# Row sums of squares by four transposes and a VectorE sum, and another order of products in the feed-forward blocks

## The chip, the core and the metric

The kernel runs on one core of a Trainium2 chip. The metric is the device time of one execution in microseconds (us), the median of several runs. All arithmetic is in fp32. In the profile PE is the matrix engine (TensorE), PEld its weight loads, DVE is VectorE, ACT is ScalarE, POOL is GpSimd and SP is the engine that issues most of the DMAs.

## The reference

The input x has four samples of 512 tokens with 256 features. Cut to what matters:

```python
# attention part, on n = layernorm(x)
q = silu(n @ Wq1 @ Wq2); a = exp(log_sigmoid(sigmoid(n @ Wk1 @ Wk2))); k = 1 - a; v = n @ Wv
h = scan over tokens of  h = a * h + k * v
out = q * h                                                     # 512 features per token
out = out * rsqrt(mean(out * out, -1) + 1e-6) * norm_w          # a sum of squares per token
x = x + layernorm(out @ Wo)
# feed-forward part, six blocks
y = layernorm(x)
for i in range(6):
    y = gelu(y @ W1[i].T + B1[i]) @ W2[i].T + B2[i] + y         # 256 -> 1024 -> 256 features
    if i < 5: y = layernorm(y) * LN_G[i] + LN_B[i]
x = x + layernorm(y)
```

## The kernel before

Features lie on the partitions and a sample's 512 tokens along the free dimension, except where a layer norm needs tokens on the partitions.

**Attention.** Each sample b is an object `Attention(b)`. `k1_q1`, `value(e)` and `scan(e)` make the four 128-feature parts e of `out` (the tile `ht`) and of its squares `sq`; GpSimd adds the four squares parts into one 128x512 tile, `self.sq[-1]`. `output(t)` multiplies the part of 128 tokens t by Wo, into one of two PSUM buffers `pt` that are used in turn. `residual()` (line 911) then needs the sum of squares of each token. It makes it by four products of a 128x128 slice of `sq[-1]` with a column of ones (line 917), which leaves a 128x4 tile in a `pt` buffer, and VectorE turns that into `ve` (line 920). A chain on GpSimd (`rstd_of`), ScalarE (`normalized`), GpSimd (the sum with x) and VectorE (`token_stats`) follows, and at its end the normalized sample is passed through DRAM (`passage`: VectorE block transposes, one store and four loads by SP) into the feature layout, where `ffn_input` picks it up. The sample's work is interleaved with that of the next one.

**Feed-forward.** The four samples go in two groups g of two samples (1024 tokens). For each block i and group g, an object `Hidden(i, g)` makes the hidden layer by 26 block products in place of 32, in the way of Strassen's method: `A_SUMS` are sums of blocks of W1, `B_SUMS` are sums of blocks of the input (both on GpSimd; `input_sums(g)` writes the tiles `tx`), and `RESULT` lists the products (p), the copies and partial sums (v) and the results (h). A line `p6 += s13 t8` is two PE products, each over one half of a 128x512 PSUM bank, added onto what the bank holds. A line `v14 = p6` is a ScalarE copy of the bank (line 497), a line `v13 = v8 + p6` a VectorE sum (line 514) that reads the bank. When both halves of a row's tokens are there, ScalarE applies gelu (line 495), and VectorE or GpSimd makes sums t1 to t4 of the gelu results. `Output(i, g, hidden)` then makes the second layer by seven groups of four products, p1 to p7, in the order of `ORDER`, and the results go through DRAM to the layer norm (`Norm`) and back to the features.

**The order.** Nothing is issued at once. Each operation is recorded in `Plan` with a cost, and `Plan.run` emits them engine by engine: whichever of an engine's ready operations has the earliest latest-start time goes first. `AFTER` is how long after the last product the other engines may end in that calculation. The order in which operations are recorded decides which buffers they get, and so what waits for what: `DEFER` is how many products of `Output` are recorded only with the next `Hidden`; `HEAD` and `BY` say how these are mixed with its first steps. Engines run their emitted instructions in order, so a waiting instruction holds up those behind it.

Of the kernel before, what the change touches and what calls it, by code (L numbers as in the profile page):

```python
# [13 lines left out]
ALU = mybir.AluOpType  # L14
PSUM = bass.MemoryType.PSUM

P = 128
# [2 lines left out]
RMS_EPS = 1e-6  # L20
LAST_PARTS = (2 * P, 2 * P)
LAST_COLUMNS = (P, P)
ORDER = "p1 p2 p6 p7 p5:0 p4 p5:1 p5:23 p3".split()
LAST_ORDER = "p1 p2 p6 p7 p4 p5".split()
DEFER = 4
HEAD, BY = 1, (2, 1)
POOLROWS = (1, 2)
AFTER = 10.0
LAST_WAYS = "POOL POOL ACT DVE DVE".split()
WARM = 5  # L30
FIRST = ((0,), (1,), (2, 3))
# [7 lines left out]
s1 = a10 + a11  # L39
# [7 lines left out]
s9 = s3 + a31  # L47
s10 = s4 - a20
s11 = s6 - s0
s12 = s2 - a01  # L50
s13 = s5 + a10
s14 = a30 - s3
s15 = s2 + a21
s16 = a30 + a20
s17 = s4 - a00
s18 = a11 - a21
# [4 lines left out]
t1 = b13 - b12  # L61
# [3 lines left out]
t5 = b03 - t2  # L65
t6 = b02 - t0
t7 = b00 + b01
t8 = b03 - t1
t9 = b11 - t1
t10 = t7 - t1  # L70
t11 = b02 - t8
t12 = t2 - t3
t13 = t3 - b03
t14 = b00 - t5
t15 = b13 - b03
t16 = b12 - t6
t17 = b10 - t4
# [3 lines left out]
RESULT = """  # L81
p0 = a21 b10
v1 = p0
p4 = a20 b00
v8 = p4
h20 = v1 + p4
p1 = s1 t1
v2 = p1
p2 = s8 b12
v3 = p2  # L90
v4 = v2 - p2
p0 += s15 t2
v5 = p0
p3 = s0 t3
# [5 lines left out]
p3 += s2 t12  # L100
v10 = v6 - p3
p4 += s10 t7
h21 = v9 - p4
h22 = v10 + p4
p3 += a20 t13
h23 = v5 - p3
v12 = p3
p5 = a00 b00
# [3 lines left out]
p7 = s3 t0  # L112
v16 = v1 - p7
h11 = v15 + p7
p6 = s5 t15
v13 = v8 + p6
v14 = p6
p8 = a01 b10
h00 = v11 + p8
p9 = s7 b11  # L120
h01 = v15 + p9
p7 += s9 t6
v17 = p7
p6 += s13 t8
h13 = v4 + p6
p7 += s14 b02
h31 = v7 - p7
v20 = p7
p5 += s18 t17
h10 = v16 + p5  # L130
p6 += a10 t11
h12 = p6 - v3
v18 = v17 + p6
p8 += s12 t5
v19 = v12 + p8
h33 = v19 - v14
p8 += s16 t14
h30 = p8 - v13
p11 = s11 b03
h03 = v19 + p11  # L140
p10 = a31 t16
# [117 lines left out]
class Plan:  # L259
# [32 lines left out]
    def latest(self):  # L292

        last = [1e9] * len(self.ops)
        at = sum(cost for engine, cost, *_ in self.ops if engine == "PE")
        end = at + AFTER
        for n in reversed(range(len(self.ops))):
# [59 lines left out]
def kernel(  # L357
# [27 lines left out]
    nc = tc.nc  # L385
    B, S, E = x.shape
    HD, E2 = wq2.shape
    NB, _, HID = w1t.shape
    NT = S // P
# [12 lines left out]
    plan = Plan()  # L402
# [7 lines left out]
    def tile_of(name, shape):  # L410
        return tiles(name, shape)[0]
# [8 lines left out]
    ones = tile_of("ones", [P, 1])  # L420
# [81 lines left out]
    def on(engine):  # L502
        return {"DVE": nc.vector, "POOL": nc.gpsimd}[engine]

    def tt(engine, dst, a, b, alu):
        cost = 0.14 + 0.00213 * dst.size if engine == "POOL" else 0.07 + 0.00104 * dst.size
        if alu == ALU.pow:
            cost = 0.29 + 0.18 * dst.size
        elif engine == "DVE" and not in_psum & {id(v.bufs[0]) for v in (a, b)}:
            cost += 0.4  # L510
        plan.op(
            engine,
            cost,
            lambda: on(engine).tensor_tensor(dst.ap, a.ap, b.ap, alu),  # L514
            [a, b],
            [dst],
        )

    def tscalar(engine, dst, src, s0, s1, op0, op1=None):
        by = [s.ap if isinstance(s, View) else s for s in (s0, s1)]  # L520
        kw = {} if op1 is None else {"op1": op1}
        cost = 0.15 + 0.003 * dst.size if engine == "POOL" else 0.07 + 0.001 * dst.size
        plan.op(
            engine,
            cost,
            lambda: on(engine).tensor_scalar(dst.ap, src.ap, *by, op0, **kw),  # L526
            [src, *(s for s in (s0, s1) if isinstance(s, View))],
            [dst],
        )
# [11 lines left out]
    def product(dst, lhs, rhs, start):  # L541

        plan.op(
            "PE",
            max(0.858 * rhs.size / 512, 0.224),
            lambda: nc.tensor.matmul(  # L546
                dst.ap, lhs.ap, rhs.ap, start=start, stop=True, skip_group_check=True
            ),
            [lhs, rhs],
            [dst],  # L550
        )

    def transpose(dst, src):
        plan.op(
            "PE",
            0.107,
            lambda: nc.tensor.transpose(dst.ap, src.ap, ident.ap),  # L557
            [src],
            [dst],
        )  # L560
# [13 lines left out]
    def store(dst, src, engine="SP"):  # L574
        queue = nc.sync if engine == "SP" else nc.scalar
        kept = isinstance(dst, View)
        to = dst.ap if kept else dst
        plan.op(
            engine,
            0.45,  # L580
            lambda: queue.dma_start(out=to, in_=src.ap),
            [src],
            [dst] if kept else [],
            src.size * P * 4 / 0.26e6,
        )
# [101 lines left out]
    def token_stats(mv, src, t):  # L687

        st = sts.next()

        def emit():
            nc.vector.bn_stats(st.ap, src.ap)  # L692
            nc.vector.bn_aggr(mv.ap[:, t, :], st.ap)  # L693

        plan.op("DVE", 0.55, emit, [src], [st, mv])

    def rstd_of(mv, to, of=None, lo=0, hi=NT, negative=True):

        ve, r, nm, nb = (to[:, k, lo:hi] for k in range(4))
        if of is None:  # L700
            tscalar("POOL", ve, mv[:, lo:hi, 1], LN_EPS, None, ALU.add)
        else:
            tt("POOL", ve, of[:, lo:hi], mv[:, lo:hi, 1], ALU.add)
        tt("POOL", r, ve, neg_half[:, lo:hi], ALU.pow)
        if not negative:
            return r
        tscalar("POOL", nm, mv[:, lo:hi, 0], -1.0, None, ALU.mult)
        tt("POOL", nb, nm, r, ALU.mult)
        return r, nb

    def normalized(src, by, t):

        r, nb = by
        z = nns.next()
        to = z
        if len(src.ap.shape) == 3:
            to = z.with_ap(z.ap.rearrange("p (f r) -> p f r", r=src.ap.shape[2]))
        act(to, src, AF.Identity, nb[:, t : t + 1], r[:, t : t + 1])
        return z
# [66 lines left out]
    class Attention:  # L786
# [124 lines left out]
        def residual(self):  # L911

            pss = pts.next()
            for t in range(NT):
                product(pss[:, t : t + 1], self.sq[-1][:, ts(t, P)], ones, True)
            hts.back(*self.grids)
            ve = rs.next()[:, 0, :]
            tscalar(  # L920
                "DVE",
                ve,
                pss[:, :NT],
                LN_EPS / E2,
                LN_EPS * RMS_EPS,
                ALU.mult,
                ALU.add,
            )
            by = rstd_of(self.mv, rs.next(), of=ve)
            mv1 = mvs.next()  # L930
            for t in range(NT):
                z = normalized(self.y[t // 2][:, t % 2, :], by, t)
                x1 = xs[self.b][t]
                tt("POOL", x1, x1, z, ALU.add)
                token_stats(mv1, x1, t)
                store(kept[self.b][t], x1)
            self.x1_by = rstd_of(mv1, rs.next())
# [115 lines left out]
    class Output:  # L1053


        def __init__(self, i, g, hidden, cols=slice(0, S), parts=None):
# [10 lines left out]
            self.x = xts[g]  # L1067
            order = LAST_ORDER if self.ending else ORDER
            self.left = [(part[:2], int(j)) for part in order for j in part[3:] or "0123"]
# [272 lines left out]
    for i in range(NB):  # L1342
        for g in range(NG):
# [32 lines left out]
            for u in range(4):  # L1376
                output.take(2)
                norm.features(u)
            output.take(len(output.left) - DEFER)
            of = (i, g)  # L1380
# [69 lines left out]
```

## Time and profile before

| | |
|---|---|
| median of 3 runs | 678.9 us (678.58 to 680.04) |
| the profiled execution's own time | 679.37 us |
| its span in the profile | 677.6 us |
| PE busy | 667.7 us, 99% of the span |
| POOL, DVE, ACT busy | 562.1, 458.6 and 357.8 us |
| mean granted PE clock | 0.997 |
| products with the column of ones | 16, as 32 matmul records of 128x1 |
| transposes by PE | 32 records of 128x128 |

A product in fp32 is two matmul records in the profile, a transpose is one. The records overlap, since they are pipelined: a 512 column record lasts 592 ns but the next one starts 429 ns later. What PE costs is therefore read from start to start and not from the durations. A label such as `bank<-tx,sa` says which tile is written from which; all products have line 546, all transposes line 557, most VectorE and GpSimd sums line 514.

### The profile page before, as it was taken

To read this page: it belongs to the slowest core of one execution; us is meant where nothing else is said; L and a number is where in the kernel's file an instruction comes from. 1 tells how busy PE (TensorE), PEld (TensorE's weight loads), DVE (VectorE), ACT (ScalarE), POOL (GpSimd) and SP (SyncE) were. 2 spreads that over 40 slices of the span, in tenths; PEclk is the share of its full clock that TensorE was granted. 3 is DMA by queue.
4 is the path that set the end of the run, shared out by engine and by line. 5 is a ranking of instruction groups with operands and counts; after the bars stand their busy time and mean duration, and the time that the engine had idled before them with its cause. 6 is when DMAs were issued, how large, how long until landed. Compare 5 with 4: busy or idle time off the path is not lost.

```text
span 677.6 us, 8284 instructions
## 1 busy us (share of the span) xinstructions
PE 667.7 (99%) x2406; PEld 445.8 (66%) x2406; DVE 458.6 (68%) x878; ACT 357.8 (53%) x625; POOL 562.1 (83%) x718
## 2 busy tenths in 40 slices
PE   8999999999999999999999999999999999999995
PEld 7565558747648558467476485584674764855884
DVE  5567665866937848649569378496495693784955
ACT  3847767635725646438257256364382572563631
POOL 4999569967999859998589998599985899885874
PEclk9999999999999999999999999999999999999998
DMA  7500522134253141550432531516504306216501
GB/s 229 192 1 32 155 63 78 48 125 124 81 184 108 56 160 34 196 164 14 145 105 92 180 101 57 161 33 202 162 10 141 107 31 190 91 65 189 151 32 63
DMA packets 81838, 73.74 MB, mean 109 GB/s; under 512 B 6272, under 2 KB 70784, under 8 KB 81792
## 3 DMA queue, kind: packets, MB, share of 16 engines
q1 hardware_dynamic: 81504, 72.94, 33.6%
q8 instruction: 19, 0.31, 0.2%
q10 hardware_dynamic: 288, 0.26, 0.1%
q14 instruction: 27, 0.22, 0.1%
HBM read 43.82 MB, written 29.36 MB: 108 GB/s over the span
## 4 chain that ended last, share of the span: by engine, by line
PE 96%; ACT 1%; DMA 1%; DVE 1%; SPq 0%; issue 0%; POOLq 0%; DVEq 0%; POOL 0%
PE bank L546 91%; PE pt L546 5%; DMA w<-in_wv 1%; ACT ht L495 0%; SPq L568 0%; ACT n L495 0%; DVE st L692 0%; PE bank L557 0%; PE pt L557 0%; DVE bank L526 0%; DVE n L536 0%; DVE mv L693 0%; DVE ht L514 0%; POOLq L1446 0%; ACT tmp L497 0%
## 5 line engine op out<-in xcount | busy, mean ns | idle before, releaser
L546 PE MATMUL bank<-tx,sa 128*128 128x256 f32 x672 | 160.9, 379 | 0.0
L497 ACT COPY tmp<-bank 128x512 f32<-128x512 f32 x144 | 83.7, 583 | 143.4 <-PE bank L546 128.1
L546 PEld LDWEIGHTS bank<-tx,sa 128*128 128x128 f32 x672 | 127.5, 190 | 22.2 <-issue 3.8
L514 DVE TENSOR_TENSOR ht<-tmp,bank 128x512 f32<-128x512 f32 x156 | 101.0, 678 | 35.2 <-ACT tmp L497 17.4
L514 POOL TENSOR_TENSOR tc<-ht,tc 128x512 f32<-128x512 f32 x96 | 121.4, 1279 | 4.1 <-ACT ht L495 3.2
L495 ACT ACTIVATE ht<-ht,b 128x512 f32<-128x512 f32 x168 | 112.9, 714 | 15.8 <-DVE ht L514 14.5
L546 PE MATMUL bank<-tc,w 128*128 128x512 f32 (+1 forms) x216 | 95.2, 577 | 0.0
L546 PE MATMUL bank<-ht,sb 128*128 128x512 f32 (+2 forms) x208 | 88.1, 555 | 0.0
L546 PE MATMUL bank<-tc,sb 128*128 128x512 f32 (+2 forms) x208 | 86.7, 556 | 0.0
L514 DVE TENSOR_TENSOR tmp<-tmp,bank 128x512 f32<-128x512 f32 x96 | 63.5, 677 | 32.2 <-PE bank L546 17.9
L536 DVE SCALAR_TENSOR_TENSOR tmp<-bank,b,xt 128x512 f32<-128x512 f32 (+1 forms) x52 | 36.5, 702 | 71.6 <-PE bank L546 71.6
L546 PE MATMUL bank<-ht,w 128*128 128x512 f32 (+1 forms) x200 | 83.8, 568 | 0.3 <-ACT ht L495 0.3
L514 POOL TENSOR_TENSOR tx<-xt,tx 128x256 f32<-128x256 f32 x108 | 76.0, 732 | 0.9
L546 PEld LDWEIGHTS bank<-tc,sb 128*128 128x128 f32 x208 | 39.2, 190 | 42.9 <-issue 41.6
L546 PEld LDWEIGHTS bank<-tc,w 128*128 128x128 f32 x216 | 40.7, 190 | 39.9 <-issue 37.3
L495 ACT ACTIVATE n<-x,r 128x256 f32<-128x256 f32 x90 | 47.9, 588 | 34.7 <-POOL r L514 34.7
L546 PEld LDWEIGHTS bank<-ht,w 128*128 128x128 f32 x200 | 37.3, 190 | 39.4 <-issue 28.7
L514 POOL TENSOR_TENSOR tx<-xt 128x256 f32<-128x256 f32 x24 | 17.5, 729 | 53.8 <-ACT xt L495 44.5
L546 PEld LDWEIGHTS bank<-ht,sb 128*128 128x128 f32 x208 | 39.0, 190 | 33.2 <-issue 31.6
L546 PE MATMUL bank<-tx,w 128*128 128x256 f32 (+1 forms) x240 | 57.4, 366 | 0.5 <-DMA w<-in_wv 0.5
L514 DVE TENSOR_TENSOR tmp<-bank,tmp 128x512 f32<-128x512 f32 (+2 forms) x54 | 35.3, 654 | 24.2 <-PE bank L546 17.9
L546 PE MATMUL bank<-xt,sa 128*128 128x256 f32 x192 | 49.3, 379 | 0.0
(94 smaller groups left out, 1029.8 us busy)
## 6 DMA issues: line engine op xcount, KB each, us to landing
x<-passed SPq DMA_DIRECT2D x120, 128.0 KB, 3.0
passed<-x SPq DMA_DIRECT2D x16, 512.0 KB, 2.6
passed<-x SPq DMA_DIRECT2D x28, 256.0 KB, 2.3
room<-passed SPq DMA_DIRECT2D x56, 128.0 KB, 3.1
w<-in_w1t SPq DMA_DIRECT2D x6, 1024.0 KB, 4.9
w<-in_w2t SPq DMA_DIRECT2D x6, 1024.0 KB, 5.7
passed<-room SPq DMA_DIRECT2D x16, 256.0 KB, 2.1
passed<-room SPq DMA_DIRECT2D x6, 512.0 KB, 2.6
```

Source lines behind the costliest of these rows:

```text
L495: lambda: nc.scalar.activation(dst.ap, src.ap, func, **kw)
L497: else nc.scalar.copy(dst.ap, src.ap),
L514: lambda: on(engine).tensor_tensor(dst.ap, a.ap, b.ap, alu),
L536: lambda: nc.vector.scalar_tensor_tensor(dst.ap, a.ap, by, b.ap, op0, op1),
L546: lambda: nc.tensor.matmul(dst.ap, lhs.ap, rhs.ap, start=start, stop=True, skip_group_check=True),
```

## The change

In `residual()` the four products with ones become four transposes of the same slices, which fill a whole 128x512 PSUM buffer with tokens on the partitions, and VectorE sums over the 128 columns of each of the four parts into `ve`. Then the scaling by constants runs on `ve` in place. The list of products, `ORDER`, `DEFER`, `HEAD`, `BY` and `AFTER` change as well, which gives every engine another order in the feed-forward blocks; the products themselves are the same.

```diff
-ORDER = "p1 p2 p6 p7 p5:0 p4 p5:1 p5:23 p3".split()
+ORDER = "p1 p2 p6 p5:0 p7 p5:123 p4 p3".split()
-DEFER = 4
-HEAD, BY = 1, (2, 1)
+DEFER = 3
+HEAD, BY = 2, (4, 1)
-AFTER = 10.0
+AFTER = 6.0
...
 p0 = a21 b10
 v1 = p0
+p1 = s1 t1
+v2 = p1
 p4 = a20 b00
 v8 = p4
 h20 = v1 + p4
-p1 = s1 t1
-v2 = p1
...
 p4 += s10 t7
+h22 = v10 + p4
 h21 = v9 - p4
-h22 = v10 + p4
...
 p6 = s5 t15
 v13 = v8 + p6
 v14 = p6
+p6 += s13 t8
+h13 = v4 + p6
 p8 = a01 b10
 h00 = v11 + p8
+p7 += s9 t6
+v17 = p7
+p5 += s18 t17
+h10 = v16 + p5
 p9 = s7 b11
 h01 = v15 + p9
-p7 += s9 t6
-v17 = p7
-p6 += s13 t8
-h13 = v4 + p6
+p8 += s12 t5
+v19 = v12 + p8
+h33 = v19 - v14
+p6 += a10 t11
+h12 = p6 - v3
+v18 = v17 + p6
+p8 += s16 t14
+h30 = p8 - v13
 p7 += s14 b02
 h31 = v7 - p7
 v20 = p7
-p5 += s18 t17
-h10 = v16 + p5
-p6 += a10 t11
-h12 = p6 - v3
-v18 = v17 + p6
-p8 += s12 t5
-v19 = v12 + p8
-h33 = v19 - v14
-p8 += s16 t14
-h30 = p8 - v13
 p11 = s11 b03
 h03 = v19 + p11
...
             for t in range(NT):
-                product(pss[:, t : t + 1], self.sq[-1][:, ts(t, P)], ones, True)
+                transpose(pss[:, ts(t, P)], self.sq[-1][:, ts(t, P)])
             hts.back(*self.grids)
             ve = rs.next()[:, 0, :]
+            by_tile = pss.ap.rearrange("p (t f) -> p t f", f=P)
+            plan.op(
+                "DVE",
+                0.07 + 0.00104 * S,
+                lambda: nc.vector.tensor_reduce(
+                    out=ve.ap, in_=by_tile, op=ALU.add, axis=mybir.AxisListType.X
+                ),
+                [pss],
+                [ve],
+            )
             tscalar(
                 "DVE",
                 ve,
-                pss[:, :NT],
+                ve,
                 LN_EPS / E2,
                 LN_EPS * RMS_EPS,
                 ALU.mult,
```

## The prediction

> **What bounds the kernel now.** I read the page first, then PE's timeline at a few places, then the chain that ended last and the timelines of the engines around it.
>
> ```profile
> PE 667.7 (99%) x2406; PEld 445.8 (66%) x2406; DVE 458.6 (68%) x878; ACT 357.8 (53%) x625; POOL 562.1 (83%) x718
> ```
>
> PE is the bound, and the page cannot say how tightly, because records overlap. I therefore compared start to start: in long runs of equal records a 512 column record costs 0.429 us, a 256 column one 0.2155 and a transpose 0.109. With these, PE loses time after its first products only at the places named below; its last record starts at 670.35 us, and the 7.2 us behind it belong to DVE, POOL and the last stores. So a microsecond less on PE is a microsecond, unless something else is late then. PE's timeline at a residual of sample 0, and at two sets of transposes in sample 1's first norm:
>
> ```profile
> 47.26 1.45 PE L546 MATMUL bank<-tc,w 128*128 128x512 f32 x3
> 48.55 0.95 PE L546 MATMUL pt<-ones,ht 128*128 128x1 f32 x8
> 49.36 1.96 PE L546 MATMUL bank<-tc,w 128*128 128x512 f32 x4
> ...
> 23.59 0.60 PE L557 MATMUL pt<-ident,n 128*128 128x128 f32 x4
> 24.03 1.88 PE L546 MATMUL bank<-tc,w 128*128 128x512 f32 x4
> 25.75 0.60 PE L557 MATMUL pt<-ident,n 128*128 128x128 f32 x4
> ```
>
> The first column is the start. The four products with ones hold PE from 48.55 to 49.36, 0.81 us, and the four records behind them take 1.96 where they take 1.88 behind transposes: 0.89 us in all. Four transposes hold it from 23.59 to 24.03, 0.44 us.
>
> The largest hole in the middle of the run is at the first output products of block 0, group 0:
>
> ```profile
> 131.34 2.74 PE L546 MATMUL bank<-ht,w 128*128 128x512 f32 x6
> 134.36 2.84 PE L546 MATMUL bank<-ht,w 128*128 128x512 f32 x6 [0.29 <-ACT ht L495]
> ```
>
> Six records should end their turn at 131.34 + 6 x 0.429 = 133.91, the next starts at 134.36: 0.45 us lost, and 0.10 in the next six (2.84 for 2.74). The chain that ended last says why:
>
> ```profile
> 126.86 0.70 DVE ht L514
> 127.56 0.02 issue
> 127.58 0.59 ACT tmp L497
> 128.17 1.49 ACT n L495 x3
> 129.65 2.09 ACT ht L495 x4
> ```
>
> ScalarE's queue is full of norms and gelus there, and the gelu of `h30`, the last product's result, comes last. `p1:3` waits for it.
>
> **The change part by part.** Sums are against the profiled execution's own 679.37 us (span 677.6, 1.8 around it); the median of the runs is 678.9, 0.47 less.
>
> *Transposes.* Four residuals, 0.89 - 0.44 = 0.45 us less each: **-1.8 us**. All four stand where PE is never idle. The rows are of the same instruction with another source tile, so I take the price as firm to 0.1 us each. Against it speaks the Trainium skill, "TensorE: Matmul & The Clock Gate", Part 4: about 275 ns for a transpose in a kernel, and a transpose does not keep PE's clock up. The trace has 272 to 301 ns as duration but 109 ns from start to start, and the windows around the transposes at 22 to 27 us show a granted clock of 1.00. By the page's 275 ns the sixteen would cost 4.4 us, which is more than the 3.6 they replace; the trace decides.
>
> *VectorE's sum.* Four new instructions of 128x512 from PSUM. No row shows this operation. A statistics instruction over 128x256 takes 413 ns, an elementwise one on 128x512 from PSUM 678, a scan over 128x512 1212; between 0.4 and 1.2 I take 0.68, as the row with the same elements and source. It lengthens the residual's chain by that. Queued behind it on DVE are `stt`, `tt` and `scan` of the next sample, whose banks PE wants 4.3 to 5.9 us after they are free, and in sample 3 `v15`, needed 3.45 us after the transposes and ready about 1.6 after them. So on PE's path: 0. The pt buffer is held longer: the next user but one, `output(1)` of the next sample, comes 3.0 us after the transposes, against 0.3 + 0.68. The chain ends in sample 1's features, which the first hidden products read. There PE waits for `ffn_input1` with 0.42 us to spare, but that ScalarE copy starts at 101.78 behind three scan activations, while its data landed at 100.5. In the new order it goes ahead of them, and GpSimd does sample 1's second norm ahead of two `input_sums`. PE comes there 1.3 us earlier plus 0.86 for `p1` being moved up. Bounds 0 to 0.8; I take **+0.3** together with the same chain of samples 2 and 3 at group 1.
>
> *Block 0's hole.* In the new list `p8 += s16 t14` stands before `p7 += s14 b02`, `p11` and `p10`. So `h30` and `h31` have 1.7 to 2.2 us more before p1 starts, and their gelu is queued ahead of the others'. Laid out on the rows (0.6 us per sum, 0.7 per gelu), it is ready 1.2 us before `p1:3`. **-0.55** (0 to -0.55). What is late next there is GpSimd's t2 for `p6:0`, by the same rows 1.2 us early.
>
> *The last block.* Between 638 and 649 us PE loses 0.43 us at five waits of the same kind, for example at `h30`:
>
> ```profile
> 643.34 2.99 PE L546 MATMUL bank<-ht,w 128*128 128x256 f32 x12
> 646.17 0.59 PE L546 MATMUL pt<-ht,w 128*128 128x256 f32 x2
> ```
>
> Twelve records should be done at 645.93; PE goes on at 646.17. The waits for `h30`, `h13` and `v19` get 0.4 to 0.9 us more room; one for `v14` comes in. **-0.3** (0 to -0.43). Behind it the order on PE and DVE from the first `finish` on is the old one, and the 7.2 us after PE's last record stay. `AFTER` only sets priorities.
>
> *A new wait.* `p6 += s13 t8` moves up by one product pair, in front of `p9`: it now stands 1.72 us behind `p6 = s5 t15` in place of 2.59. Before it may add to the bank, DVE (`v13`) and ACT (`v14`) must both have read it, and the trace shows them one after the other:
>
> ```profile
> 306.85 0.39 DVE L692 BATCH_NORM_STATS2 st<-x 128x6 f32<-128x256 f32 x1
> 307.28 0.18 DVE L693 BATCH_NORM_AGGREGATE mv<-st 128x2 f32<-128x6 f32 x1
> 307.38 1.25 DVE L514 TENSOR_TENSOR tmp<-tmp,bank 128x512 f32<-128x512 f32 x2
> 308.66 0.59 ACT L497 COPY tmp<-bank 128x512 f32<-128x512 f32 x1 [0.65 <-DVE tmp L514]
> ```
>
> The product's second record pair ends its turn on PE at 307.46. Two statistics hold DVE until 307.38, then come `v16` and `v13`, then the copy, until 309.25: 1.79 us, where 1.72 will be there. With a hand-off of 0.05 PE stands 0.12 us. The same two statistics stand there in the new order of blocks 1 to 5, group 0: five times 0.12, **+0.6** (0 to 1.5 if one more statistics pair, 0.6 us, gets in twice or thrice). In group 1 `v14` is first and 2.15 us are there for 1.7. Behind PE's wait are `p5 += s18`, then `p9`, with 0.3 us to spare or more.
>
> *The rest of the reorder.* `p1 = s1 t1` comes second in group 0, 3.4 us earlier. Its `t1` was ready 4.4 us before (GpSimd, after a run of `w1_sums`), and the new GpSimd order has two sums fewer ahead of it: 1 to 2.4 us left. In group 1 all of p3 now comes before the next block, which starts with `p2 = s8 b12` and `p1`, on the last features to land; `b12` was ready 3.66 us before its product, which comes 2.6 us earlier. The loads for it are now issued first of the two samples', so I count nothing. The weight load of W2 and the stores keep their places in SP's queue but for one: sample 3's features are collected behind the store of `p5:3`, which I reckon 1.1 us early.
>
> Sum: -1.8 + 0.3 - 0.55 - 0.3 + 0.6 = -1.75. The profiled execution would be 677.6, the median 678.9 - 1.75 = **677.1 us**. With every term at its best end (-1.8 - 0.55 - 0.43) it is 676.1.
>
> **The rivals.**
>
> *The new waits eat the gain.* The terms of +0.3 and +0.6 at 0.8 and 1.5, and nothing won in the last block: -1.8 + 0.8 - 0.55 + 1.5 = -0.05, 678.85 us; halfway, 678.0. For it: in the profile before, GpSimd and DVE stand hardly a microsecond ahead of PE in many places (0.17 us at `p2:0`, 0.34 at `p1 += a21 t9`), so small shifts show. Against it: the places are few, and most leads in the new order are as long or longer.
>
> *The hidden blocks wait at `p6 += s13 t8` everywhere.* This is the way to slower. If norm statistics stand in front of `v13` in all eleven blocks from block 0, group 1 on, at 0.56 us each, PE waits 0.12 + 0.56 = 0.68 in each: 7.5 us, for a total of 678.9 - 1.75 - 0.6 + 7.5 = 684.0. It decides from 0.34 us per block on, where 11 x 0.34 = 3.7 outweighs the other terms (-2.35) by 0.2%. Against it: in the new DVE order only two statistics come directly before `v16` and `v13` in group 0, as before, and none does in group 1.
>
> *The transposes don't overlap.* If one costs its whole duration of 0.275 us, term one becomes 4 x (1.10 - 0.89) = +0.8: 678.9 + 0.85 = 679.75. Against it are the rows at 23.59 and 25.75.
>
> **How the numbers follow.** 0.2% is 1.36 us, about what a measurement of this kernel can tell from no change. The forecast, 676.1 to 677.5, gets 0.60, the eaten gain 0.27, the wait everywhere 0.10, transposes without overlap 0.03. Faster is the first alone: 0.60. Within 0.2% (677.54 to 680.26) are the second and the fourth: 0.29, less a little for worse mixes: 0.28. Slower: 0.12. The range runs from the best end, 676.1, less 0.1 for the measurement, to the eaten gain at 678.8.
>
> **What would show it.** PE has 32 records fewer of 128x1 and 16 more transposes, 2390 in all, and four transposes take 0.44 us from start to start at each residual. The record behind `h30` at 134.36 shows no wait, and the last block's holes are at most 0.15. At `p6 += s13 t8` in group 0 a hole of about 0.1 appears. Four reductions of some 0.7 us are on DVE. The prediction is wrong if PE's span without holes is not 1.8 shorter, or if new holes, above all at a start of a hidden block, add up to more than 1.2 us.

## The result, and the profile after

The changed kernel takes 680.37 us (median of 20 runs, 679.85 to 681.09) and the kernel before 679.15 us (median of 20, 678.58 to 680.04). The ratio is 1.0016, with a 95% interval from 1.0010 to 1.0021: slower by about 1.2 us, where the prediction had 1.8 us faster. The profiled execution took 680.61 us, with a span of 678.8. The engines' line of the page:

```profile
PE 668.9 (99%) x2390; PEld 443.0 (65%) x2390; DVE 460.2 (68%) x882; ACT 357.7 (53%) x625; POOL 560.4 (83%) x718
```

PE has the 2390 records foretold. The removal came out as worked out. Here is PE's timeline at a residual, at the first output products of block 0, and VectorE's new row among the groups of instructions (span, share, then busy us and mean ns):

```profile
48.47 0.60 PE L557 MATMUL pt<-ident,ht 128*128 128x128 f32 x4
48.91 1.88 PE L546 MATMUL bank<-tc,w 128*128 128x512 f32 x4
...
130.03 6.17 PE L546 MATMUL bank<-ht,w 128*128 128x512 f32 x14
```

```profile
L924 DVE TENSOR_REDUCE r<-pt 128x4 f32<-128x512 f32 x4 | 2.7, 675 | 0.7 <-PE pt L557 0.7
```

The transposes hold PE for 0.44 us and the records behind them take 1.88. Fourteen output products run on without a hole (13 x 0.429 + 0.59 = 6.17), where six products ended in 0.45 us of waiting before. What the prediction did not have stands in the hidden blocks. The same place comes back in each of blocks 1 to 5, group 0; here it is in block 2, first on PE, at the output products p6 (p6:0 is the first of the group's four products, p6:3 the fourth):

```profile
323.84 2.78 PE L546 MATMUL bank<-tc,sb 128*128 128x512 f32 x6
326.77 1.98 PE L546 MATMUL bank<-tc,sb 128*128 128x512 f32 x4 [0.15 <-POOL tc L514]
```

Six records should end their turn at 323.84 + 6 x 0.429 = 326.41, and the next starts at 326.77: 0.36 us, and the four behind it take 1.98 where 1.88 is usual. (0.04 of it is a wait at p6:0, ahead of the second record.) The wait is for a `tc` of GpSimd. Its timeline in the kernel after, and then the same stretch of the kernel before:

```profile
319.70 1.27 POOL L514 TENSOR_TENSOR ht<-ht 128x512 f32<-128x512 f32 x1
321.06 0.41 POOL L526 TENSOR_SCALAR r<-mv 128x4 f32<-128x4 f32 x2
321.44 1.04 POOL L514 TENSOR_TENSOR r<-r,neg_half 128x4 f32<-128x4 f32 x1
322.45 1.27 POOL L514 TENSOR_TENSOR tc<-ht,tc 128x512 f32<-128x512 f32 x1
323.68 1.00 POOL L514 TENSOR_TENSOR r<-r,neg_half 128x4 f32<-128x4 f32 x1
...
325.44 4.97 POOL L514 TENSOR_TENSOR tc<-ht,tc 128x512 f32<-128x512 f32 x4
```

```profile
314.15 1.04 POOL L514 TENSOR_TENSOR r<-r,neg_half 128x4 f32<-128x4 f32 x1
...
320.73 5.09 POOL L514 TENSOR_TENSOR tc<-ht,tc 128x512 f32<-128x512 f32 x4
...
327.33 1.04 POOL L514 TENSOR_TENSOR r<-r,neg_half 128x4 f32<-128x4 f32 x1
```

The lines with `neg_half` are the powers of two layer norms, one per sample. Before, one (314.15) ran ahead of the hidden block's last sums and the other (327.33) behind the t2 sums. After, both stand in the middle of the sums: the t2 of row 0 (322.45) has to let two TENSOR_SCALARs and a power go first, the t2 of row 3 (the first of the four at 325.44) a second power and four small instructions more. It ends at 326.71; PE goes on at 326.77.

The second new place is `p6 += s13 t8`, in the same five blocks. All engines, block 2:

```profile
306.25 1.25 DVE L514 TENSOR_TENSOR tmp<-tmp,bank 128x512 f32<-128x512 f32 x2
...
307.19 1.03 PE L546 MATMUL bank<-xt,w 128*128 128x256 f32 x4
...
307.53 0.59 ACT L497 COPY tmp<-bank 128x512 f32<-128x512 f32 x1 [0.65 <-DVE tmp L514]
...
308.26 1.32 PE L546 MATMUL bank<-tx,sa 128*128 128x256 f32 x5
```

PE's four records end their turn at 307.19 + 4 x 0.2155 = 308.05. `v13` is ready at 307.50, the copy `v14` at 308.12, and PE starts at 308.26, 0.21 us late; the next record comes 0.075 late again.

In the table, a wait is what a PE record takes from its start to the next start beyond the usual 0.429, 0.2155 or 0.109 us. The 0.08 that the record behind each set of ones takes more is no wait; it is part of the 0.89 us of a residual.

| PE's waits in us | before | after |
|---|---|---|
| block 0, group 0, hidden products | 0.0 | 0.56 |
| block 0, group 0, output products | 0.56 | 0.00 |
| blocks 1 to 5, group 0: `p6 += s13 t8` | 0.0 | 5 x 0.28 = 1.4 |
| blocks 1 to 5, group 0: p6:0 and p6:3 | 0.0 | 5 x 0.46 = 2.3 |
| last block (636 to 662 us) | 0.43 | 0.22 |

With 1.8 us of shorter records, PE's last record should start -1.8 + 0.56 - 0.56 + 1.4 + 2.3 - 0.21 = 1.7 us later; it starts at 671.97 against 670.35, 1.6 later. Behind it come 6.85 us in place of 7.2, and so the span is longer by 1.25. The traces of the other runs have 6.8 to 7.2 us there, with the old order and with the new one, so this last part is not put down to the change.

### The profile page after: what moved, and what is told of

The parts are those of the page before. It is cut to its first block, busy times and chain, and to the rows that moved or that the text cites. A ratio compares the mean times of both kernels' runs of the same rounds, so it can differ in the third digit from the quotient of the medians.

```text
span 678.8 us, 8257 instructions
## 1 busy us (share of the span) xinstructions
PE 668.9 (99%) x2390; PEld 443.0 (65%) x2390; DVE 460.2 (68%) x882; ACT 357.7 (53%) x625; POOL 560.4 (83%) x718
## 4 chain that ended last, share of the span: by engine, by line
PE 88%; POOL 7%; DVE 2%; issue 1%; ACT 1%; DMA 1%; SPq 0%; POOLq 0%; DVEq 0%; ACTq 0%
PE bank L546 83%; PE pt L546 5%; POOL tc L514 4%; POOL r L514 1%; POOL ht L514 1%; POOL r L526 1%; DMA x<-in_x 1%; ACT tmp L497 1%; PE pt L557 0%; ACT ht L495 0%; DVE ht L514 0%; DVE st L692 0%; SPq L568 0%; PE bank L557 0%; DVE mv L693 0%
## 5 line engine op out<-in xcount | busy, mean ns | idle before, releaser
L546 PE MATMUL bank<-tc,sb 128*128 128x512 f32 (+2 forms) x208 | 88.1, 559 | 0.8 <-POOL tc L514 0.8
L546 PE MATMUL bank<-xt,sa 128*128 128x256 f32 x192 | 51.1, 379 | 0.0
```

What stands on the lines that cost most here:

```text
L546: lambda: nc.tensor.matmul(dst.ap, lhs.ap, rhs.ap, start=start, stop=True, skip_group_check=True),
```

## The experiments

The theory (A): the transposes are worth their 1.8 us, and the new orders of GpSimd and VectorE in blocks 1 to 5, group 0, cost 3.7. The rivals: VectorE's sum is what costs (B); an order that eases one place makes the norms late elsewhere (C); PE is paced by something later, so that time won comes back as another wait (D).

| | us, median | ratio to before, 95% | PE's waits, 170 to 636 us |
|---|---|---|---|
| e1 transposes only | 681.06 | 1.0020 to 1.0038 | 4.33 |
| e2 reorder only | 681.92 | 1.0024 to 1.0050 | 3.64 |
| e3 norms behind t2, sorted anew | 681.43 | 1.0018 to 1.0037 | 4.78 |
| e4 `p6 += s13` later in the list | 680.34 | 1.0006 to 1.0024 | 3.72 |
| e5 transposes, old order | 677.49 | 0.9966 to 0.9983 | 0.0 |
| e6 t2 moved | 683.91 | 1.0056 to 1.0081 | 7.60 |
| e7 statistics moved | 682.88 | 1.0041 to 1.0066 | 6.42 |
| e8 both | 686.95 | 1.0096 to 1.0127 | 10.31 |
| e9 t2 and stt moved | 678.76 | 0.9985 to 1.0003 | 1.94 |
| e10 `v15` ahead | 680.81 | 1.0015 to 1.0032 | 4.30 |
| e11 e9 and e10 | 679.23 | 0.9992 to 1.0010 | 3.17 |
| e12 e11 and block 0 | 679.97 | 1.0001 to 1.0019 | 2.83 |
| e13 e11 and `v19` ahead | 677.76 | 0.9972 to 0.9990 | 1.94 |

In the last column the kernel before has 0.0 and the kernel after 3.73; in e9 and e13 about 0.2 of it is the last block's first wait, which starts ahead of 636 us there. The runs were timed in four series, each with the kernel before beside it, whose median was 679.06 to 679.32.

**e1, e2: each half of the change alone.** e1 is the kernel before with this; e2 is the kernel after without it.

```diff
-                product(pss[:, t : t + 1], self.sq[-1][:, ts(t, P)], ones, True)
+                transpose(pss[:, ts(t, P)], self.sq[-1][:, ts(t, P)])
...
+            plan.op(
+                "DVE",
+                0.07 + 0.00104 * S,
+                lambda: nc.vector.tensor_reduce(
...
```

> The kernel before with the four transposes and VectorE's sum alone; every list and constant is the old one. Theory A (the transposes are worth their 1.8 us and the reorder loses more than that): 679.15 - 1.8 = 677.35 us, with the old holes kept (0.45 at block 0's first output products). Rival B (the VectorE sum lengthens the residuals' chains so that PE waits for them, and the loss lies there): 679 us or more, with new holes on PE between 40 and 125 us.

> The kernel after with the products with ones put back; all of the reorder stays. Theory A: 680.4 + 1.8 = 682.2 us, with the new holes in blocks 1 to 5, group 0 (0.28 us at p6 += s13 t8 and 0.46 us at the output products p6, five times each). Rival B: about 678.3 us, since the reorder by itself would win what the prediction said (0.55 + 0.3).

e2 came out as A has it, with the holes of the kernel after. The planner sorted its attention part and block 0 a little differently, but from block 1 on all engines have the order of the kernel after, and 3.64 of its 3.73 us of waits are there with the products with ones: blocks 1 to 5 do not lose by the transposes. e1 did not: 681.06 us, 3.7 above the forecast. But B's new holes are not there either: from 40 to 170 us PE waits 0.25 us, and from 170 on, where no residual is left, 4.33. They stand in hidden blocks whose code e1 does not touch. The planner sorts all engines by costs, and e1 changed two of them; PE's queue in block 1, for instance, has one half of `p4 += s10 t7` ahead of `p2`, which the kernel before has not. e1 was thus a second reorder, and e5 was needed.

**e5: the transposes with the old order kept.** The planner is given the old costs.

```diff
-                product(pss[:, t : t + 1], self.sq[-1][:, ts(t, P)], ones, True)
+                transpose(pss[:, ts(t, P)], self.sq[-1][:, ts(t, P)], 0.224)
...
+            plan.op("DVE", 0.07 + 0.001 * NT, emit, [pss], [ve])
```

> The kernel before with the four transposes and VectorE's sum, and every engine's order of before kept: the planner is told the old costs (0.224 us per transpose, VectorE's sum and scaling as one operation of 0.074), so that it sorts as before. In e1 it was told other costs and sorted the feed-forward blocks anew. Theory A (transposes are worth 1.8 us and all losses come from orders): 679.15 - 1.8 = 677.35 us, with the holes of before in their places. Rival B (VectorE's sum delays the residuals' chains, PE pays for it): 678.5 us or more, with new holes between 40 and 130 us.

677.49 us beside 679.32 for the kernel before in the same series, 1.83 less: A, and the lowest median of this study. Record by record, PE, VectorE, ScalarE and GpSimd have the order of the kernel before here. What VectorE's sum costs can be read as well. VectorE's timeline around block 0's `v15` and `v16` (the two at 120.05), then PE's at `p7 += s9 t6`, then PE's in the kernel before:

```profile
118.72 0.66 DVE L923 TENSOR_REDUCE r<-pt 128x4 f32<-128x512 f32 x1
119.42 0.17 DVE L926 TENSOR_SCALAR r<-r 128x4 f32<-128x4 f32 x1
...
120.05 1.25 DVE L514 TENSOR_TENSOR tmp<-tmp,bank 128x512 f32<-128x512 f32 x2
121.22 0.68 DVE L514 TENSOR_TENSOR ht<-tmp,bank 128x512 f32<-128x512 f32 x1
```

```profile
120.91 1.03 PE L546 MATMUL bank<-xt,sa 128*128 128x256 f32 x4
122.04 2.18 PE L546 MATMUL bank<-tx,sa 128*128 128x256 f32 x9
```

```profile
118.36 0.95 PE L546 MATMUL pt<-ones,ht 128*128 128x1 f32 x8
119.17 2.84 PE L546 MATMUL bank<-tx,sa 128*128 128x256 f32 x12
...
122.70 1.03 PE L546 MATMUL bank<-xt,sa 128*128 128x256 f32 x4
123.56 0.81 PE L546 MATMUL bank<-tx,sa 128*128 128x256 f32 x3
```

The sum stands in front of `v15`, `v16` and `h11` (121.22), for which `p7 += s9 t6` waits. PE should go on at 120.91 + 4 x 0.2155 = 121.77 and starts at 122.04; with the record behind, 0.34 us. In the kernel before it goes on at 122.70 + 4 x 0.2155 = 123.56 without a wait; the 0.08 that it has among these products (2.84 us for the twelve behind the ones) belongs to sample 3's ones. So the four sums cost 0.34 us, all of it in sample 3's.

**e3: the norms behind t2, by the planner.** GpSimd's eight norm instructions and two t4 sums get a dependency on t2.

```diff
+            if last and g == 0:
+                t4s = [hidden.rows[j].t4 for j in (0, 1)]
+                for n in norm.rstds + t4s:
+                    plan.ops[n][3].update(hidden.rows[j].t2 for j in (0, 3))
```

> The kernel after with one thing changed in GpSimd's order in blocks 1 to 5, group 0: the eight small instructions of the two layer norms and two t4 sums stand behind the t2 sums of rows 0 and 3 in place of ahead of them. No engine gets more or less work. Theory A (the two powers of about 1.0 us each and their small neighbours hold up the t2 that PE reads): the holes of 0.04, 0.32 and 0.10 us at p6 go, five times 0.46 = 2.3 us, so 678.1 us; the norms end 1.2 us later, and the next block's first products have 2.3 us to spare. Rival C (the gelus on ScalarE and VectorE's sums ahead of t2 are as late as the norms): the hole stays above 0.3 and the time is 680 or more; the same if the norms, now later, hold up the next block's start.

681.43 us. The holes at p6 in group 0 are gone and others are there: 0.46 us at the start of a block of group 1 (PE waits for an `xt` of ScalarE), 0.26 and 0.10 at p6 in group 1, and up to 0.63 at `p6 += s13 t8`. That looks like C, but the planner had sorted other instructions too, so it settles nothing.

**e4: `p6 += s13 t8` later in the list.**

```diff
-p6 += s13 t8
-h13 = v4 + p6
 p8 = a01 b10
 h00 = v11 + p8
+p6 += s13 t8
+h13 = v4 + p6
```

> The kernel after with p6 += s13 t8 and h13 put back behind p8 = a01 b10 and h00, so that again three products, 2.59 us, lie from the start of p6 = s5 t15 to the product that adds onto its bank. Theory A: the hole of 0.28 us in blocks 1 to 5, group 0 goes, five times 0.28 = 1.4 us, so 679.0 us; h13 comes 0.86 us later, but its row is not finished before h12. Rival D (PE is only paced by what comes later, the t2 sums, so that time won here is lost there): the holes at p6 grow by what is won here, and the time stays at 680.4.

680.34 us, and the hole of 0.28 is unchanged: the planner had put `p8 = a01 b10` ahead of `p6 += s13 t8` already, and PE's records have the same order in both kernels there. All four engines have the order of the kernel after, so this is the kernel after once more (680.37 there) and tells nothing of A or D. From here on the planner's queues are taken as they are in the kernel after, and single instructions are moved in them (in e6 to e8 always by a step of 1). The added code shifts the line numbers: products have line 563, sums 531, the `stt` 553, copies 514, gelus and normalized tiles 512.

```diff
+        for n, m, step in self.behind:
+            queue = queues[self.ops[n][0]]
+            queue.remove(n)
+            queue.insert(queue.index(m) + step, n)
```

**e6, e7, e8: one queue at a time.** The first line is e6, the second e7, both are e8.

```diff
+                plan.behind.append((hidden.rows[3].t2, hidden.rows[0].t2))
+                plan.behind += [(n, hidden.at["v13"]) for n in norm.stats[0][1::-1]]
```

> The kernel after with one GpSimd instruction moved in each of blocks 1 to 5, group 0: the t2 sum of row 3 stands directly behind the t2 of row 0, in front of the power of the first sample's norm and five small instructions; in e3 the planner sorted again and other places changed too, here nothing else does. Theory A: t2 ends about 1.7 us earlier, the hole of 0.42 us at p6:3 goes, five times, so 680.4 - 2.1 = 678.3 us; the 0.04 at p6:0 stays; the norms end 1.25 us later with 2.3 to spare at the next block's start. Rival C (the norms' delay holds up the next block): 0.3 us or more new at each start of a block in group 1, and 680 us or more.

> The kernel after with two VectorE statistics moved in each of blocks 1 to 5, group 0: from in front of v16 and v13 to directly behind v13; nothing else moves. e4 was meant to ease the same wait, but there the planner emitted the products of these blocks in the order it had before. Theory A: v13 ends 0.4 us or more earlier, the copy v14 behind it too, and the hole of 0.28 us at p6 += s13 t8 goes, five times: 680.4 - 1.4 = 679.0 us. Rival D (PE is paced by the later t2 sums): the holes at p6 grow by as much, 680.4 us.

> e6 and e7 together. Theory A: the two holes are separate, the gains add: 680.4 - 2.1 - 1.4 = 676.9 us, 2.3 us under the kernel before, with no hole above 0.1 us left in the hidden blocks behind block 0. Rival D (pacing): about 678.3, no more than e6.

All three went the wrong way, by 3.5, 2.5 and 6.6 us against the kernel after. In e6 the hole at p6:3 is gone (PE's timeline, then VectorE's):

```profile
324.01 5.34 PE L563 MATMUL bank<-tc,sb 128*128 128x512 f32 x12
330.28 1.98 PE L563 MATMUL bank<-ht,sb 128*128 128x512 f32 x4 [0.93 <-DVE tmp L553]
```

```profile
327.89 0.71 DVE L763 STREAM_TRANSPOSE room<-n 128x512 f32<-128x512 f32 x1 [2.99 <-ACT n L512]
328.88 0.71 DVE L763 STREAM_TRANSPOSE x<-n 128x512 f32<-128x512 f32 x1 [0.27 <-ACT n L512]
329.51 0.71 DVE L553 SCALAR_TENSOR_TENSOR tmp<-bank,b,xt 128x512 f32<-128x512 f32 x1
```

Twelve records without a hole, and then 1.1 us lost at p7:0. It adds onto the bank that the `stt` (VectorE's SCALAR_TENSOR_TENSOR) at 329.51 reads, and that `stt` stands behind two block transposes, which wait for ScalarE's normalized tiles, which wait for GpSimd's powers. It does not need them: by PE's records the product p6:3 that it reads was done at about 327.6, some 1.9 us before the `stt` started. VectorE's idle 2.99 us lay mostly ahead of that; what cost PE time were the two transposes in front, which came late. So C holds, one step earlier than it said: not the next block, but the queue of the next engine. e7 shows the like. VectorE and PE there:

```profile
306.44 0.69 DVE L531 TENSOR_TENSOR tmp<-tmp,bank 128x512 f32<-128x512 f32 x1 [0.18 <-PE bank L563]
...
308.76 0.67 DVE L531 TENSOR_TENSOR tmp<-tmp,bank 128x512 f32<-128x512 f32 x1
...
309.57 1.10 PE L563 MATMUL bank<-tx,sa 128*128 128x256 f32 x4 [0.58 <-DVE tmp L531]
```

`v13` (306.44) comes about 0.3 us earlier against PE's records than in the kernel after and the hole at `p6 += s13 t8` is gone. But VectorE now waits for PE in front of `v16` and `v13`, 0.6 us in which the statistics ran before, and `v15` (308.76), behind three statistics, is more than 0.8 later: PE waits 0.75 at `p5 += s18 t17`. e8's loss is about the sum of both (6.6 for 6.0).

**e9: e6 with VectorE's queue mended.** The `stt` goes ahead of the transposes.

```diff
+                plan.behind.append((hidden.rows[3].t2, hidden.rows[0].t2, 1))
+                plan.behind.append((output.sn2_op, norm.passing[1], 0))
```

> e6 with one more instruction moved in each of blocks 1 to 5, group 0: VectorE's stt behind p6:3 (it reads the bank that p7:0 adds onto) goes ahead of the two block transposes of the norms' passage, which in e6 stood in front of it and waited 2.99 us for ScalarE's normalized tiles, and those for the powers on GpSimd. Theory A (GpSimd's order cost 0.46 us a block, and e6 lost its gain because the norms stand at the head of VectorE's queue too): the holes of 0.42 us at p6:3 and of 1.2 us at p7:0 are both gone, 680.4 - 2.1 = 678.3 us. Rival C (the norms are now simply too late for the next block): new holes at the starts of group 1 or behind p7:3, 680 us or more.

678.76 us, 1.6 less than the kernel after, and 2.1 less by the spans (676.7 against 678.8). PE's timeline, then VectorE's `stt`:

```profile
323.28 5.35 PE L563 MATMUL bank<-tc,sb 128*128 128x512 f32 x12
328.46 1.88 PE L563 MATMUL bank<-ht,sb 128*128 128x512 f32 x4
```

```profile
326.95 0.75 DVE L553 SCALAR_TENSOR_TENSOR tmp<-bank,b,xt 128x512 f32<-128x512 f32 x1 [2.78 <-PE bank L563]
```

Twelve records should take 12 x 0.429 = 5.15 us and take 5.18 to the next start: only the 0.04 at p6:0 is left, and the four behind it run without a hole. The `stt` now waits for PE's product alone. So GpSimd's order costs what A said: PE's waits in blocks 1 to 5 are 5 x 0.42 us less. One new wait of 0.13 us stands at the start of one block of group 1.

**e10, e11: the statistics.** e10 is the two lines, e11 is e9 and e10.

```diff
+                plan.behind.append((norm.stats[1][0], hidden.at["h11"], 1))
+                plan.behind.append((norm.stats[0][1], hidden.at["v15"], 1))
```

> The kernel after with two VectorE statistics moved in each of blocks 1 to 5, group 0: the second one of the first sample goes from in front of v16 to behind v15, and the first one of the second sample from in front of v15 to behind h11. In e7 the hole at p6 += s13 t8 was gone, but v15 came 0.8 us later and p5 += s18 t17, next on PE, waited 0.75 for it. Theory A: v13 0.35 us earlier and v15 0.9 earlier than in the kernel after; both waits gone, 680.4 - 1.4 = 679.0 us. Rival D: the time won comes back as a longer wait at p6, 680.4.

> e9 and e10 together. Theory A: 680.4 - 2.1 - 1.4 = 676.9 us, about 2.3 under the kernel before and 0.6 under e5, with no hole over 0.1 us in blocks 1 to 5, group 0. Rival D: no better than the better of the two.

Both missed. The holes at `p6 += s13 t8` and at `v15` are gone, and a new one stands at `p8 += s16 t14`, which waits for `v19`:

```profile
312.95 0.59 PE L563 MATMUL bank<-xt,sa 128*128 128x256 f32 x2
313.67 1.13 PE L563 MATMUL bank<-tx,sa 128*128 128x256 f32 x4
```

These lines are e10's. 0.28 us, and 0.10 behind it: 5 x 0.38 in place of 5 x 0.28. By two moves the wait had gone from `v13` to `v15` to `v19`. That is D's picture, if VectorE is full there. e11's profile also has 1.03 us at the start of one block of group 1, where e9 has its 0.13.

**e12: block 0.** e11, and sample 2's last statistics go behind `v19` in block 0.

```diff
+                plan.behind.append((att[2].mv1_op, hidden.at["v19"], 1))
```

> e11 and one VectorE statistics instruction of sample 2 moved in block 0, group 0, from in front of h01 to behind v19, for which p8 += s16 t14 waits 0.35 us and the record behind it 0.08. Theory A: 676.9 - 0.43 = 676.5 us. Rival C: the attention chain of samples 2 and 3, 1.1 us later, holds up block 0, group 1, whose products p2 and p1 have 1.0 us to spare: 677 or more.

The wait for `v19` went (0.15 us of waits are left among the hidden products, of 0.56), but 1.31 came at the output products: sample 2's norm on GpSimd starts later, and sample 3's behind it in the same queue; ScalarE's normalized tiles, which wait for that, stand in front of the gelus, and p1:3 and p6 wait for those. C again, in ScalarE's queue.

**e13: the statistics behind `v19`.** e11 and:

```diff
+                plan.behind.append((norm.stats[0][2], hidden.at["h12"], 1))
+                plan.behind.append((norm.stats[1][2], hidden.at["h12"], 1))
+                plan.behind.append((norm.stats[1][1], hidden.at["v19"], 1))
```

> e11 with three VectorE statistics moved in each of blocks 1 to 5, group 0: the second and third of the second sample and the third of the first go from in front of v19 to behind v19 and h12. In e11 the wait at p6 += s13 t8 was gone, but a new one of 0.28 and 0.10 us stood at p8 += s16 t14, which waits for v19. Theory A (the statistics of both norms now stand in front of v19 in place of one norm's and a half, so that whichever sum is behind them is late): the wait at v19 goes too, five times 0.38, and 679.2 - 1.9 = 677.3 us. Rival D (VectorE has no room in this stretch, a wait taken away comes back at the next sum): 679 us, with a new hole at p1 or p6 in the output products.

677.76 us, 1.5 less than e11 and 2.6 less than the kernel after: A in the main. In place of 0.38 at `v19` there is 0.14 at p1:0, and the 0.04 at p6:0 is 0.03 or less. VectorE has the same instructions in e11 and e13, so it had room; their place was at fault. Its profile also holds a wait of 0.97 us at the start of one block of group 1, for features that came late through DRAM; the other blocks have none. It is the place where e9, e11 and e12 have 0.13, 1.03 and 0.68 and the kernel after none, so it seems to come with the later norms of e9 (C, in one block); no run shows that alone. e13 beats both kernels, with an interval that overlaps e5's.

## Why the prediction was wrong

*Transposes, -1.8:* right in size. In e5, with every queue in the old order, PE stands 1.79 us earlier behind the fourth residual than in the kernel before; it loses 0.34 to VectorE's sum, and its last record starts 1.47 earlier. That the medians differ by 1.83 all the same has luck in it: of the 1.9 us between the two spans 0.4 lie behind PE's last record. The Trainium skill, "TensorE: Matmul & The Clock Gate", Part 4, has about 275 ns per transpose in one kernel's context. That is near the duration here (272 to 273 ns in e5) and not the price: e5's four transposes take 0.44 us from start to start. The granted clock of e5 from 40 to 130 us is 1.00; these transposes stand between products, so no run shows the clock in a longer stretch of them.

*VectorE's sum, +0.3:* the duration was right (0.675 us for 0.68), and the cost lies within the bounds of 0 to 0.8, but by luck, since the place was wrong: I looked for it where sample 1's features land, and in sample 3 I named `v15` alone, which has time. It is in VectorE's queue at sample 3's residual, where `v16` and `h11` stand behind `v15`. e5 has 0.34. In the kernel after the hidden products of that block have 0.56, and with ones (e2) none, but e2's engines have another order in block 0, so how much of the 0.56 is the sum's is not shown.

*Block 0's hole, -0.55, and the last block, -0.3:* right: -0.56 and -0.21. That the hole went by the moved product is not shown alone; in e1, with the old list, the planner's other order removes it too.

*The new wait, +0.6:* right in place and number of blocks, too small in size: 0.28 us each for 0.12, 1.4 in all. The chain (`v16` and `v13` 1.25, the copy 0.59) was the right one. What I sized wrong is what lies between its links: 0.05 us taken, measured 0.03 from VectorE to ScalarE, 0.14 from ScalarE to PE and 0.075 that the record behind a wait loses.

*The rest of the reorder, 0:* this is the step that failed, with 2.3 us. I laid out GpSimd's t2 on rows for block 0 only and wrote that most leads "are as long or longer". In blocks 1 to 5 the two norms of the block before lie in the same queue, and I did not place their instructions: two powers of 1.0 us and six small ones, 3.15 us ahead of row 3's t2. I had read `DEFER`, `HEAD` and `BY` only for when features land. What changed is VectorE's order of the two samples' statistics. The loads of both samples' tokens are issued together in both kernels (in block 2 from 299.18 us before, from 298.06 after). Before, all four statistics of one sample ran ahead of the other's; after, they alternate. The last one of each sample, before and then after:

```profile
312.07 0.42 DVE L692 BATCH_NORM_STATS2 st<-x 128x6 f32<-128x256 f32 x1
...
324.31 0.41 DVE L692 BATCH_NORM_STATS2 st<-x 128x6 f32<-128x256 f32 x1
```

```profile
319.13 0.41 DVE L692 BATCH_NORM_STATS2 st<-x 128x6 f32<-128x256 f32 x1
...
320.25 0.42 DVE L692 BATCH_NORM_STATS2 st<-x 128x6 f32<-128x256 f32 x1
```

A sample's power follows its last statistics. So both powers fall into the sums in place of one ahead and one behind. Which of the list, `DEFER`, `HEAD`, `BY` and `AFTER` puts them there stays open; no run tried these alone. What their place costs is shown by e9: with one t2 ahead of the second power and the `stt` ahead of the transposes, 2.1 of the 2.3 us are gone from PE's waits.

The prediction's own sign of being wrong came true: new holes of 4.3 us in the hidden blocks and at p6, where it allowed 1.2. Of the rivals, the eaten gain was the nearest: it named the thin leads of GpSimd and DVE, then priced them at the two waits already known and dismissed the others as few. They are few, but one that comes back in five blocks is worth more than the change's gain. The wait at `p6 += s13 t8` did not spread to all eleven blocks. (The chances of the second and the fourth outcome add to 0.30, not 0.29; nothing rests on it.)

## What to carry to other kernels

Where engines run their queues in order, price a reorder by the place that repeats: follow each wait back into the queue of the engine that ends it, and lay every instruction there end to end, the small ones of other stages too. A move that eases one queue lengthens what other queues wait for at their heads; e6 became a gain only when the second queue was moved with it. And where a planner sorts by costs, a change of a cost is a reorder: a part is only tested alone with the old order held.

## What had not been expected

A PE wait costs more than itself. At most holes of these traces the record behind the wait takes 0.29 to 0.32 us to the next start in place of 0.2155 (256 columns), or 0.50 to 0.53 in place of 0.429 (512 columns): 0.075 to 0.10 us more. GpSimd's power over 128x4 takes 1.00 to 1.04 us, where a product of the same shape takes 0.20 (the two at 325.14 take 0.35), nearly as long as a sum over 128x512 (1.27). The length of an engine's idle time does not tell what it costs: in e6 VectorE stood still for 2.99 us, but what PE lost, 1.1 us, came from an `stt` of 0.71 us that had its data and started about 1.9 us late behind two block transposes.
